# Small operands in PSUM, a norm queued behind a softmax, and another order in the second layer

## The chip, the cores and the metric

The kernel runs on one core of a Trainium2 chip. A core has TensorE (matrix products into PSUM), VectorE (elementwise work and reductions), ScalarE (activation functions), GpSimd[...] and SyncE, which issues most of the DMAs. In the profile they are called PE, DVE, ACT, POOL and SP; PEld are the weight loads of TensorE. The metric is the device time of one execution in microseconds (us).

## The reference

Four layers work in turn on one activation x of shape (2, 512, 32, 32), in 32-bit floats. The change touches the first two and the step into the third.

Layer 0 is a deformable attention with 8 heads of 64 channels, and a dense pair behind it. For each of the 2 x 8 pairs of batch and head, a small convolution of the queries gives offsets on an 8 x 8 grid; keys and values are sampled there, and the offsets also give the bias of the attention:

```python
off = gelu(conv(qg, off_dw_w) + off_dw_b)
off = tanh(einsum('bchw,oc->bohw', off, off_pw_w)) * 4.0
vx, vy = gx + off[:, 0], gy + off[:, 1]
nx, ny = 2.0 * vx / 7 - 1.0, 2.0 * vy / 7 - 1.0        # grid_kv
pos = grid_q[:, :, None, :] - grid_kv[:, None, :, :]
bias = sign(pos) * log1p(abs(pos))
bias = relu(bias @ cpb_w1 + cpb_b1)                    # 2 -> 128
bias = relu(bias @ cpb_w2 + cpb_b2)                    # 128 -> 128
bias = bias @ cpb_w3 + cpb_b3                          # 128 -> 1
sim = q @ k^T + bias;  out = softmax(sim) @ v
x = x + out_w @ out + out_b
x = x + mlp_w2 @ gelu(mlp_w1 @ bn(x) + mlp_b1) + mlp_b2
```

The bias is computed for every query (1024) and key (64) of every pair, with 128 hidden units: this is by far the largest part of the work.

Layer 1 is a linear attention: queries and keys (64 channels) are brought to unit length per position, k^T x and the sum of the keys are formed once per batch, and each position is divided by a sum over its query. Layer 2 begins with a group norm, whose means and variances are taken over x as layer 1 leaves it; layers 2 and 3 are softmax attentions.

## The kernel before, in words

**Layer 0.** The outer loop runs over u = 0 to 15, one head of one batch each. Within a u, o = 0 to 7 are groups of keys, and each o has two half steps. A half step is: VectorE makes the first hidden layer h1 with four operations (`first_hidden`, L705, each the sum of a table x and a table y); TensorE multiplies it by the second weights (`second_hidden`, L729) in four groups q = 0 to 3 of 16 products each, all of which read all four parts of h1; ScalarE applies bias and ReLU (L739, L741); GpSimd adds groups (L750, L753), and issues DMAs that add others. Later products reduce this to sim. The table y is written by VectorE (L690) into columns 0 to 255 of one single PSUM bank, `self.bank`, that layer 0 keeps for small things: the same bank has small statistics of the softmax (`self.joint`, columns 364 up), the product `o` of the offsets at columns 256 and 257, and now and then the sampling's weights and products.

Beside this stream, other generators are stepped at fixed places, one piece between two pieces of the stream: `attend` (bias plus q k^T, the softmax and its product with v, L785 to L869) and `offsets`, for a pair of heads at a time. There are eight such pairs; the first is computed at the start, the other seven beside u = 1, 3, 5, 7, 9, 11 and 13. The steps of `offsets` that the change touches are, in order: tanh on ScalarE (L421); three VectorE operations giving the positions of the keys and their distance from the queries, `pos` (L426, L427, L429); abs, log and sign on ScalarE (L444 to L446); on VectorE the product of log and sign (L451); a DMA of it on SyncE's queue; g on ScalarE (L457), and a DMA of it. The first pair (`bt == 0`) takes the sign in another way. The order of instructions on each engine is the order in which the generators issue them. The framework adds the waits; between different engines it treats one PSUM bank as a whole, whichever columns are touched.

**The tail of layer 0.** The last head's softmax is `attend` with u = 15: turn sim (L827), maximum (L828), four small copies (L825), L830, L831, subtract (L833), exp on ScalarE (L835), sum (L837), copies, reciprocal (L840), multiply (L842), turn (L844, into `pt`). TensorE multiplies `pt` by v (L855), copies bring it to `att` (L866, L869), and the projection follows (L255, and L895 for the last block). Then comes the dense pair, `mlp0`. It multiplies in seven products of half size, P1 to P7 (`seven`, L942), for which sums of the weights' blocks are made on GpSimd (`left_sums`) and sums of the right side's blocks on VectorE (`first_sums`, L925 and L926; `second_sums`). `norm(0)` scales x into blocks r0 to r3 with eight operations (L976) and then forms r4 and r5. In this part the framework's scheduler decides the places of `norm(0)` among the instructions around it; what follows, from the first product on, is in an order written out by hand.

**Layer 1.** The whole layer is issued in a hand-written order of helpers at L1278 to L1322, for TensorE, ScalarE and VectorE; GpSimd and SyncE are left to the scheduler. `queries_keys(b, half)` makes 16 products and an addition each (L1116, L1119) and squares after the second half (L1127). `means_less(b)` takes four negative means of x on ScalarE (L1132) into the tile `less`, cleared by a memset (L1099). `unit_length(b)` reduces, takes roots and scales (L1136 to L1141, giving `kn`). `turned_x` transposes x on TensorE (L1151), `keys_sum` sums the keys (L1160), `keys_x` forms k^T x (L1184), `centred` (L1201), `matrix` (L1224, L1234) and `result` (L1264, L1270) finish. `channel_means(2, 0, t)` (L1560, L1561), `group_means` (L1570 to L1580) and `norm_first` (L1611) already belong to layer 2's group norm; layer 2's first product, qk20P (L1428), needs what `norm_first` gives.

Of the kernel before, what the change touches and what calls it, by code (L numbers as in the profile page):

```python
# [56 lines left out]
class Net:  # L57
# [320 lines left out]
    def offsets(self, m, bt, ps):  # L378

        nc = self.nc
        b, t = divmod(bt, CT)
        if "q" not in m:
            self.normed(m, bt)
            yield
            self.queries(m, bt, ps)
            yield
        qp = m["q"]
        prod = self.fone.tile([P, 36 * NJ], F32, tag="big", name=f"prod{b}{t}")  # L390
        prod = prod.rearrange("p (a b j) -> p a b j", a=6, b=6)
        conv = self.fpool.tile([P, NJ], F32, tag="conv", name=f"conv{b}{t}")
        if bt == 0:
            yield from self.first_conv(qp, prod, conv, ps)
        else:
            for ky in range(6):
                nc.vector.tensor_tensor(
                    prod[:, ky, :, :].rearrange("p k (y x) -> p k y x", y=8),
                    self.window(qp, 6 * ky, 6),
                    self.taps[:, 6 * ky : 6 * ky + 6].unsqueeze(2).unsqueeze(3).to_broadcast([P, 6, 8, 8]),  # L400
                    ALU.mult,
                )
                if ky % 2:
                    yield
            for third in (slice(0, 24), slice(24, 44), slice(44, NJ)):
                nc.vector.tensor_reduce(
                    conv[:, third], prod[:, :, :, third].rearrange("p a b j -> p j (a b)"), AX.X, ALU.add
                )
                yield
        ge = self.fpool.tile([P, NJ], F32, tag="ge", name=f"ge{b}{t}")  # L410
        nc.scalar.activation(ge, conv, AF.Gelu, bias=self.col("dw_b"))
        if bt == 0:
            next(self.weights)
        yield
        yield from self.odd()
        o = self.bank[:, 256:258]
        for par in range(2):
            rows = slice(par * DH, (par + 1) * DH)
            nc.tensor.matmul(o[rows, :], lhsT=ge[rows, :], rhs=self.colr("pw", 2)[rows, :], start=True, stop=True)
        at = self.fpool.tile([P, 2], F32, tag="at", name=f"at{b}{t}")  # L420
        nc.scalar.activation(at, o, AF.Tanh)  # L421
        if bt == 0:
            early = self.fpool.tile([P, 1], F32, tag="early", name="early_ln")
            nc.scalar.activation(early, self.cols[:, 0:1], AF.Ln, scale=0.0, bias=1.0)
        yield
        nc.vector.scalar_tensor_tensor(at, at, 4.0, self.grid[:, G_KEY : G_KEY + 2], ALU.mult, ALU.add)  # L426
        nc.vector.tensor_scalar(at, at, 2.0 / 7.0, -1.0, ALU.mult, ALU.add)  # L427
        pos = self.fpool.tile([P, 2, W], F32, tag="pos", name=f"pos{b}{t}")
        nc.vector.tensor_tensor(  # L429
            pos,  # L430
            self.grid[:, G_QRY : G_QRY + W].unsqueeze(1).to_broadcast([P, 2, W]),
            at.unsqueeze(2).to_broadcast([P, 2, W]),
            ALU.subtract,
        )
        yield
        log = self.fpool.tile([P, 2, W], F32, tag="log", name=f"log{b}{t}")
        if bt == 0:

            nc.vector.scalar_tensor_tensor(log, pos, -1.0, pos, ALU.mult, ALU.max)
            nc.vector.tensor_scalar(pos, pos, 0.0, 2.0, ALU.is_ge, ALU.mult)  # L440
            next(self.weights)
            nc.scalar.activation(log, log, AF.Ln, bias=1.0)
        else:
            nc.scalar.activation(log, pos, AF.Abs)  # L444
            nc.scalar.activation(log, log, AF.Ln, bias=1.0)
            nc.scalar.activation(pos, pos, AF.Sign)  # L446
        yield
        if bt == 0:
            nc.vector.scalar_tensor_tensor(log, pos, -1.0, log, ALU.add, ALU.mult)
        else:  # L450
            nc.vector.tensor_tensor(log, log, pos, ALU.mult)  # L451
        logs = self.dram.tile([P, 2 * W], F32, tag="logs", name=f"logs{b}{t}")
        nc.sync.dma_start(logs, log.rearrange("p d x -> p (d x)"))
        spots = self.dram.tile([P, 2], F32, tag="spots", name=f"spots{b}{t}")

        g = self.fpool.tile([P, 2], F32, tag="g", name=f"g{b}{t}")
        nc.scalar.activation(g, at, AF.Identity, scale=W / 2.0, bias=self.grid[:, G_MID : G_MID + 1])  # L457
        nc.sync.dma_start(spots, g)
        m["log"], m["logs"], m["spots"] = log, logs, spots
        yield  # L460
# [343 lines left out]
    def attend(self, u, m, sim, att, ps):  # L804
# [36 lines left out]
        yield True  # L841
        nc.vector.tensor_tensor(t, t, joint.unsqueeze(2).to_broadcast([P, 2 * NB, W]), ALU.mult)  # L842
        pt = self.soft.tile([P, HF], F32, tag="pt", name=f"pt{u}")
        nc.vector.transpose(pt, t.rearrange("p a k -> p (a k)"))  # L844
        yield

        if ps:
# [15 lines left out]
        for c in range(2):  # L863
            at = slice(c * DH, (c + 1) * DH)
            if ps:
                nc.scalar.copy(to[:, :, c, :], o[at, :, 0 : HF // 2])  # L866
            else:
                nc.scalar.copy(to[:, 0, c, :], parts[0][at, :])
                nc.vector.tensor_copy(to[:, 1, c, :], parts[1][at, :])  # L869
        yield True  # L870

    def project_block(self, acc, att, w, bias: str, b: int, o: int, out):
# [74 lines left out]
    def mlp0(self):  # L947
# [5 lines left out]
        with ExitStack() as ctx:  # L953
# [16 lines left out]
            def norm(b):  # L970

                r = [xpool.tile([P, 2, HF], F32, tag=f"r{i}", name=f"mx{b}{i}") for i in range(7)]
                for i in (0, 3, 2, 1):
                    for k in range(2):
                        t = 2 * (i // 2) + k
                        vec.tensor_scalar(  # L976
                            r[i][:, k, :],
                            self.xs[b][t][:, (i % 2) * HF : (i % 2 + 1) * HF],
                            s2[:, t : t + 1],
                            self.col("bn2_b", t),  # L980
                            ALU.mult,
                            ALU.add,
                        )
                        yield r
                self.first_sums(vec, r)
                if b > 0:
                    self.second_sums(vec, r)
                yield r

            for xn in norm(0):  # L990
                pass
            ready = weights(0)
            with self.tc.manual_schedule(engines={getattr(mybir.EngineType, e) for e in ("PE", "Activation", "DVE")}):
                for n in range(B * CT):
# [86 lines left out]
    def layer1(self, w, bias):  # L1081
# [3 lines left out]
        with ExitStack() as ctx:  # L1085
# [10 lines left out]
            vec, act, gps = nc.vector, nc.scalar, nc.gpsimd  # L1096
            spare = pool.tile([P, N], F32, tag="spare", name="l1spare")
            less = pool.tile([P, CT, 32], F32, tag="less", name="l1less")
            gps.memset(less, 0.0)  # L1099
            pick = pool.tile([P, B], F32, tag="pick", name="l1pick")  # L1100
            gps.tensor_tensor(pick, self.ident[:, 0:B], self.ident[:, 32 : 32 + B], ALU.add)
            for at in (64, 96):
# [26 lines left out]
            def means_less(b):  # L1129

                for t in range(CT):
                    act.activation(spare, self.xs[b][t], AF.Copy, scale=-1.0 / N, accum_out=less[:, t, b : b + 1])  # L1132
# [145 lines left out]
            self.first = {2: self.first_block(2, 0)}  # L1278
            engines = {getattr(mybir.EngineType, e) for e in ("PE", "Activation", "DVE")}
            with self.tc.manual_schedule(engines=engines):  # L1280
                queries_keys(0, 0)
                means_less(0)
                queries_keys(0, 1)
                queries_keys(1, 0)
                unit_length(0)
                means_less(1)
                queries_keys(1, 1)
                keys_sum(0)
                turned_x(0, range(NB))
                unit_length(1)  # L1290
                divided(0)
                keys_x(0)
                row = means_row()
                turned_x(1, range(0, 4))
                centred(0)
                keys_sum(1)
                turned_x(1, range(4, NB))
                matrix(0)
                turned(0, 0)
                turned(0, 1)  # L1300
                means_columns(row)
                divided(1)
                for j in range(2):
                    for h in range(2):
                        result(0, j, h)
                keys_x(1)
                for t in (0, 2):
                    self.channel_means(2, 0, t)
                turned(1, 0)
                turned(1, 1)  # L1310
                centred(1)
                for t in (1, 3):
                    self.channel_means(2, 0, t)
                matrix(1)
                steps = self.group_means(2, 0, ps_m.tile([P, 2, 5 * CT], F32, tag="s", name="gm2"))
                result(1, 0, 0)
                next(steps)
                result(1, 0, 1)
                next(steps, None)
                result(1, 1, 0)  # L1320
                self.norm_first(2)
                result(1, 1, 1)  # L1322

# [790 lines left out]
```

## Time and profile before

| | |
|---|---|
| median of 3 runs | 3247.07 us (3243.41 to 3247.81) |
| profiled execution, its own time | 3249.37 us |
| span in the profile | 3247.6 us |
| TensorE busy | 3223.4 us (99%), mean granted clock 0.998 |
| VectorE busy | 2427.2 us (75%) |
| ScalarE busy | 1960.6 us (60%) |
| GpSimd busy | 2355.6 us (73%) |
| first bias product to last of layer 0's 16,384 | 23.2 to 1913.8 us |
| first product of the dense pair | 1954.84 us |
| first product of layer 2 | 2396.68 us |

Times inside the profile are counted from the start of its span, and the profiled execution's own time is 1.8 us longer than the span. A row of a group gives line, engine, operation, tiles written and read, shapes, count, and behind the first bar busy time in all and mean ns of one, behind the second the idle time just before and what ended it. In the timeline each row gives start, length, engine, line and tiles, and the idle time before it in brackets. The clock is the share of full speed that TensorE was granted.

### The profile page before, as it was taken

The page shows a single profiled execution, that of the slowest core. Times are in us where ns is not written, and L with a number is a line of the kernel's source. Part 1 is how long each engine was busy: PE and PEld are TensorE (multiplying, and loading weights), DVE is VectorE, ACT ScalarE, POOL GpSimd, SP SyncE. Part 2 cuts the span into 40 slices and gives each one's busy share as a digit, 9 for nine tenths or more (in the row PEclk, how much of TensorE's full clock was granted, in tenths as well). Part 3 has the DMA queues.
Part 4 walks back from the last instruction along what each step waited for, and adds up shares of the span by engine and source line. Part 5 has one row for each costly group of instructions (what it writes and reads, how often), then busy time and mean ns, then how long its engine had stood idle before and what let it go on. Part 6 is the DMA issues. An engine that isn't in the chain of part 4 may idle for free.

```text
span 3247.6 us, 58820 instructions
## 1 busy us (share of the span) xinstructions
PE 3223.4 (99%) x24188; PEld 1221.3 (38%) x24188; DVE 2427.2 (75%) x2745; ACT 1960.6 (60%) x2032; POOL 2355.6 (73%) x1559
## 2 busy tenths in 40 slices
PE   9999999999999999999999999999999999999999
PEld 4343323322233333333433334444555533455333
DVE  7878888878877678878877755575465689855897
ACT  7787887887877688887887742111131466213662
POOL 7999999999988699999989954433333458634575
PEclk9999999999999999999999999999999999999999
DMA  6787777777777577777877752111000100000001
GB/s 178 160 170 160 167 167 161 167 157 167 164 161 148 122 166 160 169 162 162 168 163 166 160 152 78 47 39 39 1 1 1 40 1 1 14 1 14 1 1 53
DMA packets 94349, 341.88 MB, mean 105 GB/s; under 512 B 16625, under 2 KB 18801, under 8 KB 78897
## 3 DMA queue, kind: packets, MB, share of 16 engines
q0 software_dynamic: 52832, 232.82, 37.2%
q1 hardware_dynamic: 40224, 103.06, 9.9%
q8 instruction: 195, 3.19, 0.4%
q10 hardware_dynamic: 1008, 2.08, 0.2%
q14 instruction: 90, 0.73, 0.1%
HBM read 67.36 MB, written 4.46 MB: 22 GB/s over the span
## 4 chain that ended last, share of the span: by engine, by line
PE 84%; DVE 10%; POOL 4%; issue 2%; ACT 1%; DMA 1%; DVEq 0%; POOLq 0%; ACTq 0%; SPq 0%
PE hp L729 46%; PE s L1653 5%; PE o L1682 5%; DVE h L705 3%; PE qk20P L1428 1%; PE qk30P L1428 1%; PE m_5P L942 1%; PE m_3P L942 1%; PE m_2P L942 1%; PE m_0P L942 1%; PE qk31P L1428 1%; PE qk21P L1428 1%; PE m_6P L942 1%; PE m_4P L942 1%; PE m_1P L942 1%
## 5 line engine op out<-in xcount | busy, mean ns | idle before, releaser
L729 PE MATMUL hp<-h,w2s 128*32 128x512 f32 x16384 | 1795.2, 592 | 2.1 <-DVE h L705 1.0
L705 DVE CUSTOM_DVE_ANT_1 h<-tx,bank 128x1024 f32<-128x1024 f32 (+1 forms) x1028 | 1180.8, 1212 | 261.8 <-PE hp L729 197.0
L739 ACT ACTIVATE h<-hp,magb 128x1024 f32<-128x1024 f32 x1024 | 1132.7, 1110 | 370.2 <-PE hp L729 368.5
L729 PEld LDWEIGHTS hp<-h,w2s 128*32 128x32 f32 x16384 | 558.6, 110 | 1200.2 <-issue 1123.7
L753 POOL TENSOR_TENSOR h<-h,h 128x1024 f32<-128x1024 f32 x254 | 723.9, 2850 | 0.0
L750 POOL TENSOR_TENSOR h<-h,h 128x1024 f32<-128x1024 f32 x255 | 718.7, 2818 | 1.5 <-ACT h L739 1.5
L1657 ACT ACTIVATE e<-s 128x1024 f32<-128x1024 f32 x256 | 261.8, 1024 | 181.1 <-PE s L1653 177.2
L746 POOL DMA_DIRECT2D h<-h x255 | 269.7, 1058 | 119.9 <-ACT h L739 116.3
L741 ACT ACTIVATE h<-h,flip 128x1024 f32<-128x1024 f32 x256 | 294.4, 1150 | 8.4
L1682 PE MATMUL o<-e,v 64*64 64x512 f32 x2048 | 265.3, 589 | 2.2 <-DVE q L1721 2.2
L1653 PE MATMUL s<-q,k 64*64 64x512 f32 x2048 | 266.0, 591 | 0.0
L1664 POOL TENSOR_TENSOR some<-some,e 128x1024 f32<-128x1024 f32 x64 | 167.7, 2620 | 26.4 <-ACT e L1657 23.8
L1662 POOL TENSOR_TENSOR some<-e,e 128x1024 f32<-128x1024 f32 x32 | 76.1, 2378 | 141.7 <-DVE sum L1671 102.4
L765 POOL DMA_DIRECT2D h<-h x124 | 141.5, 1141 | 21.0 <-DMA h<-h 19.2
L1669 DVE TENSOR_TENSOR sum<-sum,e 128x1024 f32<-128x1024 f32 x64 | 124.0, 1938 | 29.5 <-ACT e L1657 26.8
L912 POOL TENSOR_TENSOR mlp_w<-mlp_w 128x512 f32<-128x512 f32 x16 | 21.1, 1318 | 169.8 <-DMA mlp_w<-in_mlp_w 153.0
L755 POOL DMA_DIRECT2D h<-h x127 | 109.1, 859 | 39.0 <-POOL h L753 37.2
L1682 PEld LDWEIGHTS o<-e,v 64*64 64x64 f32 x2048 | 77.9, 133 | 145.0 <-issue 135.1
L1653 PEld LDWEIGHTS s<-q,k 64*64 64x64 f32 x2048 | 76.6, 133 | 133.1 <-issue 117.2
L1003 ACT ACTIVATE mh<-mh,cols 128x512 f32<-128x512 f32 x64 | 46.1, 721 | 124.3 <-DVE mh L1021 63.6
L1416 POOL TENSOR_TENSOR sq<-q 128x512 f32<-128x512 f32 x32 | 33.3, 1039 | 99.2 <-DVE q L1435 55.1
L1667 DVE TENSOR_TENSOR sum<-e,e 128x1024 f32<-128x1024 f32 x32 | 80.9, 2527 | 32.0 <-ACT e L1657 32.0
(583 smaller groups left out, 3328.1 us busy)
## 6 DMA issues: line engine op xcount, KB each, us to landing
h<-h POOLq DMA_DIRECT2D x382, 512.0 KB, 5.5
lb<-logs SPq DMA_DIRECT2D x63, 512.0 KB, 6.6
h<-h POOLq DMA_DIRECT2D x124, 256.0 KB, 3.7
sum<-h SPq DMA_DIRECT2D x248, 128.0 KB, 3.3
mlp_w<-in_mlp_w SPq DMA_DIRECT2D x16, 1024.0 KB, 4.9
x<-in_x SPq DMA_DIRECT2D x8, 512.0 KB, 7.9
qkw<-in_l_qk SPq DMA_DIRECT2D x2, 2048.0 KB, 7.9
out<-x SPq DMA_DIRECT2D x15, 256.0 KB, 2.0
```

What stands on the lines that cost most here:

```text
L705: self.nc.vector._custom_dve(TENSOR_ADD_SAT, out=h1[r][:, k, cut, :], in0=x[:, 4 * half + 2 * r + k, :].unsqueeze(1).to_broadcast([P, H // ...
L729: nc.tensor.matmul(hp[rows, cut], lhsT=self.l0w2[:, 32 * q : 32 * q + 32], rhs=h1[k][:, cut], start=True, stop=True)
L739: nc.scalar.activation(y, hp, AF.Relu, bias=self.magb[:, q, 0:1])
L741: nc.scalar.activation(y, y, AF.Copy, scale=self.flip)
L746: nc.gpsimd.dma_start(y, ys[0], accum_op=ALU.add)
L750: (nc.vector if final else nc.gpsimd).tensor_tensor(y, y, ys[2], ALU.add)
L753: (nc.vector if final else nc.gpsimd).tensor_tensor(z, z, other, ALU.add)
L942: self.nc.tensor.matmul(acc[p], lhsT=w[:, a, k, p * P : (p + 1) * P], rhs=right(r, k), start=k == 0, stop=k == 1)
L1653: nc.tensor.matmul(s[halves[c], par, :], lhsT=ks[p][rows, at : at + DH], rhs=qs[p][rows, cut], start=True, stop=True)
L1657: nc.scalar.activation(e, s, AF.Exp, scale=DH**-0.5)
L1664: nc.gpsimd.tensor_tensor(state["some"], state["some"], e, ALU.add)
L1682: nc.tensor.matmul(o[halves[par], r, :], lhsT=v[n // 2][rows, n % 2, at : at + DH], rhs=e[rows, par, :], start=(n == 0), stop=(n == NB - 1),)
```

## The change

There are three parts.

1. In `offsets`, the result of tanh and the tile `at` (scaled offset and key position) lie in `self.bank`, columns 258 to 261, and the sign lies there at columns 384 to 447, where the sampling's weights and products also lie at other times. VectorE's operations at L426, L427, L429 and L451 so read one operand from PSUM. `log` and `pos` stay in SBUF.
2. `norm(0)` of the dense pair is no longer free to be placed anywhere: its first two operations are issued behind the last softmax's turn (L844), the other six and the two sums behind VectorE's copy at L869.
3. In layer 1, the memset of `less` is on VectorE; `means_less(0)` comes first; half of `turned_x(0)` comes ahead of `keys_sum(0)`; the channel means of t = 1 come ahead of `turned(1)` and `centred(1)`; the first step of the group means comes ahead of the first `result(1)`, and `norm_first(2)` ahead of both `result(1, 1)`.

```diff
-        at = self.fpool.tile([P, 2], F32, tag="at", name=f"at{b}{t}")
-        nc.scalar.activation(at, o, AF.Tanh)
+        tanh, at = self.bank[:, 258:260], self.bank[:, 260:262]
+        nc.scalar.activation(tanh, o, AF.Tanh)
...
-        nc.vector.scalar_tensor_tensor(at, at, 4.0, self.grid[:, G_KEY : G_KEY + 2], ALU.mult, ALU.add)
+        nc.vector.scalar_tensor_tensor(at, tanh, 4.0, self.grid[:, G_KEY : G_KEY + 2], ALU.mult, ALU.add)
...
-            nc.scalar.activation(pos, pos, AF.Sign)
+            sign = self.bank[:, 384:448].rearrange("p (d x) -> p d x", d=2)
+            nc.scalar.activation(sign, pos, AF.Sign)
...
-            nc.vector.tensor_tensor(log, log, pos, ALU.mult)
+            nc.vector.tensor_tensor(log, log, sign, ALU.mult)
...
-        nc.vector.transpose(pt, t.rearrange("p a k -> p (a k)"))
+        self.weights_turned = nc.vector.transpose(pt, t.rearrange("p a k -> p (a k)"))
...
-                nc.vector.tensor_copy(to[:, 1, c, :], parts[1][at, :])
+                self.values_out = nc.vector.tensor_copy(to[:, 1, c, :], parts[1][at, :])
...
-            for xn in norm(0):
-                pass
+            first_norm = norm(0)
+            with self.tc.issue_after(self.weights_turned.ins):
+                for _ in range(2):
+                    next(first_norm)
+            with self.tc.issue_after(self.values_out.ins):
+                for xn in first_norm:
+                    pass
...
-            gps.memset(less, 0.0)
+            vec.memset(less, 0.0)
...
+                means_less(0)
                 queries_keys(0, 0)
-                means_less(0)
                 queries_keys(0, 1)
...
                 queries_keys(1, 1)
+                turned_x(0, range(0, 4))
                 keys_sum(0)
-                turned_x(0, range(NB))
+                turned_x(0, range(4, NB))
...
-                for t in (0, 2):
+                for t in (0, 2, 1):
                     self.channel_means(2, 0, t)
                 turned(1, 0)
                 turned(1, 1)
                 centred(1)
-                for t in (1, 3):
-                    self.channel_means(2, 0, t)
+                self.channel_means(2, 0, 3)
                 matrix(1)
                 steps = self.group_means(2, 0, ps_m.tile([P, 2, 5 * CT], F32, tag="s", name="gm2"))
+                next(steps)
                 result(1, 0, 0)
-                next(steps)
+                next(steps, None)
                 result(1, 0, 1)
-                next(steps, None)
-                result(1, 1, 0)
                 self.norm_first(2)
-                result(1, 1, 1)
+                for h in range(2):
+                    result(1, 1, h)
```

## The prediction

> **What bounds the kernel now.** I read the page's first, fourth and fifth parts, then the by-form groups of VectorE, then each of the three places in time.
>
> ```profile
> PE 3223.4 (99%) x24188; PEld 1221.3 (38%) x24188; DVE 2427.2 (75%) x2745; ACT 1960.6 (60%) x2032; POOL 2355.6 (73%) x1559
> PE 84%; DVE 10%; POOL 4%; issue 2%; ACT 1%; DMA 1%; DVEq 0%; POOLq 0%; ACTq 0%; SPq 0%
> L729 PE MATMUL hp<-h,w2s 128*32 128x512 f32 x16384 | 1795.2, 592 | 2.1 <-DVE h L705 1.0
> ```
>
> TensorE is the bound: 99% busy, 84% of the chain. Only what lets it start sooner, or run at full clock, counts. One half step of the offsets' bias (64 products L729) takes it 6.86 us, and VectorE's share of it is four L705 at about 1.15 us, 4.62 in all, so VectorE has 2.2 us over per half step.
>
> VectorE's groups with their forms (busy and mean ns behind the bar):
>
> ```profile
> L451 DVE TENSOR_TENSOR log<-log,pos 128x64 f32<-128x64 f32 x7 | 36.3, 5183 | 0.0
> L429 DVE TENSOR_TENSOR pos<-grid,at 128x64 f32<-128x64 f32 x8 | 21.7, 2712 | 0.3
> L426 DVE SCALAR_TENSOR_TENSOR at<-at,grid 128x2 f32<-128x2 f32 x8 | 6.9, 863 | 0.4 <-ACT at L421 0.4
> L831 DVE TENSOR_SCALAR bank<-bank,cols 128x16 f32<-128x16 f32 x16 | 3.9, 243 | 0.5
> ```
>
> An operation over 64 columns takes 5.2 us while L831 on 16 columns takes 0.24. Those two SBUF inputs wait for something. In u = 3, VectorE's timeline and then TensorE's L729 alone in four stretches of half a step (busy us, matmuls, weight loads, clock, DMA share, GB/s):
>
> ```profile
> 412.64 0.68 DVE L833 TENSOR_TENSOR t<-t,bank 128x512 f32<-128x512 f32 x1
> 413.24 7.17 DVE L451 TENSOR_TENSOR log<-log,pos 128x64 f32<-128x64 f32 x1
> 420.33 4.60 DVE L705 CUSTOM_DVE_ANT_1 h<-tx,bank 128x1024 f32<-128x1024 f32 x4
> ```
>
> ```profile
> 407.50:414.36 6.86, 6.86 (x68) 2.08 (x64) 1.00 0.89 205
> 421.23:428.09 6.86, 6.41 (x42) 1.43 (x42) 1.00 0.87 162
> 428.09:434.95 6.86, 6.86 (x72) 2.07 (x68) 1.00 0.57 135
> ```
>
> Behind the 7.17 the next h tile ends at 424.93; TensorE wants all four parts of it within 1.3 us of 421.23. It makes 42 products in the stretch, not 64: 22 x 0.107 = 2.4 us. From start to start the loss is 2.92.
>
> The tail of layer 0 and the clock of layer 1 (TensorE's timeline with the idle time before; stretches with the columns PE, weight loads, DVE, ACT, POOL, clock, DMA, GB/s; ScalarE's timeline):
>
> ```profile
> 1937.41 0.69 PE L855 MATMUL bank<-pt,v 64*64 64x256 f32 x2 [4.28 <-DVE pt L844]
> 1937.40:1944.00 6.60, 6.59 (x15) 2.68 (x16) 0.85 (x2) 0.73 (x2) 0.31 (x1) 0.53 0.68 242
> 2346.79 1.06 ACT L1132 ACTIVATE l1spare<-x 128x1024 f32<-128x1024 f32 x1 [27.17 <-POOL l1less L1099]
> 2355.12 2.28 PE L1160 MATMUL kb<-kn,l1ones 128*128 128x64 f32 x16 [1.29 <-DVE kn L1140]
> 2355.00:2362.20 7.20, 7.08 (x50) 6.95 (x50) 3.47 (x6) 6.40 (x11) 1.27 (x1) 0.76 0.01 2
> 2387.60:2396.70 9.10, 6.74 (x22) 2.79 (x21) 5.78 (x18) 3.20 (x6) 3.70 (x3) 0.81 0.00 0
> 2396.68 1.52 PE L1428 MATMUL qk20P<-xn,qkw 128*128 128x512 f32 x3 [1.20 <-DVE xn L1611]
> ```
>
> TensorE waits 4.28 us for the last softmax, then runs at 0.53 of its clock. In layer 1 it waits for kn, for the matrices and for the first xn, at 0.76 and 0.81.
>
> [...] GpSimd's sums L750 and L753 take 2.82 and 2.85 us and L451 takes 1.42 to 7.17; L429 of the first pair, with GpSimd not summing yet, takes 0.24, the later seven 3.07. [...] VectorE's L705, idle 23.8 us for ScalarE's L421 and 28.8 for L583, which share the bank with y. [...] The trace: half clock for 6.83 us (1936.78 to 1943.6) behind the 4.28, and for 3.41 twice in layer 1.
>
> **Part by part.**
>
> *Offsets (seven pairs; the eighth, the first in time, is at the start).* L426, L429 and L451 now have one input in SBUF and one in PSUM. I price them at the uncontended rows: 0.16, 0.24 and 0.24. VectorE loses (6.9 - 1.3) + (21.7 - 1.9) + (36.3 - 1.7) = 60 us of work, nearly all of it hidden under TensorE. What is not hidden, from the starts of the groups of 16 products beyond 1.716 us with no other matmul between: 1.59 in u = 1, and 0.44 + 2.48 in each of u = 3, 5, 7 and 13; none in 9 and 11. 1.59 + 4 x 2.92 = 13.3 us. This is the ceiling.
>
> The new waits: sign lies in the bank that y, h's input, lies in, so ScalarE's sign waits for the h tile before it, VectorE's next reader waits for sign, ScalarE's g waits for the log product, and the next h tile waits for g. Worked for u = 3: L426 to L429 end near 391.7 instead of 395.1. Sign ends at 402.2 as before (ReLU, abs, a table load of 1.28, Ln stand ahead of it), so h_210 runs 402.2 to 406.8, two us later than before; TensorE's limit is 407.5 + 1.3. The softmax group (2.6) and y (0.49) follow to 410.0; h_300 ends at 414.7, limit 415.7. The subtraction and the product end at 415.6, g at 416.05, h_310 at 420.7, limit 422.5. No stall is left. For u = 1, h_110 ends at 160.7 against 161.0; for u = 9 the y of the sixth step now waits for sign (1184.25) and h_600 ends at 1189.5 against 1189.4. I take 0.8 off for these two: **12.5**, range 5 (two thirds of a us lost at each h tile behind sign and g) to 13.3. The first pair's g00 now precedes TensorE's L320 in the same bank: at most 0.3, in the 0.8. On SP's queue, logs and spots of one pair change places with a sum DMA; they are wanted a whole u later.
>
> *The dense pair's norm.* Before, eight L976 (0.55 each) and the two sums L925/L926 (1.22 each) lie between the softmax's operations. Without them the chain from 1924.4 is 0.71 + 0.61 + 0.80 + 0.21 + 0.27 + 0.60 + 0.78 (exp) + 0.69 + 0.83 + 0.21 + 0.30 + 0.72 + 0.75 = 7.5, so pt is at 1931.9 instead of 1937.36, before TensorE is done with its ob products at 1932.98. The wait of 4.28 goes, and with it the half clock: 6.83 us at half rate are 3.4 us of work lost. Less 0.3 for the seam: **7.4**. The norm now runs after the copies (1934.9): six L976 to 1937.7, the residual additions L264 between, the sums after; r4 and r5 are wanted by P6 at about 1950, r0 by P1 at 1947.3. The weights' DMA on SP and GpSimd's left sums move forward with L855 (landing 4.8 us, then 4 x 1.32 by about 1944). If that cover fails, P1 or P6 waits, at most for what was gained. Bounds 4 (the half clock stays) and 8.
>
> *Layer 1.* Memset of less on VectorE instead of behind GpSimd's three sums of 2.35: means(0) can begin at 2340.5 instead of 2346.79 and is done before queries_keys(0, 1); sq0 follows the addition at 2347.4 instead of 2351.39. kn(0) is ready near 2353.4 instead of 2354.97, before TensorE ends its products at 2353.83; sixteen transposes then stand ahead of kb. keys_x(0) begins at about 2359.45 instead of 2362.17: 2.7, of which the half clock is 1.7. GpSimd's later pieces keep their order. In the second half, channel means of t = 1 come before m1c, so m1c is 0.26 later, but mat(1) no longer waits for those of t = 3, and norm_first precedes two of the four result groups on VectorE: first xn some 3.5 us sooner, now 2396.54. Sum **6.2**; 3 if an idle 1.3 us again brings the half clock (1.7), 7 at the most.
>
> *Sum.* 12.5 + 7.4 + 6.2 = 26.1. The profiled execution took 3249.37 us, 1.8 more than its span of 3247.6: 3223.3 there. The median of the runs is 3247.07, 2.3 below the profiled one: **3221.0**. Whether the median or the profiled time is the typical one is worth 2 us either way.
>
> **Rivals.** *The bank takes back [...]* (0.19; its extreme, that PSUM operands do not shorten the operations, included): waits for sign and g stall TensorE [...]. For it: seven pairs, and tables are loaded ahead of sign; against it: 2 us of slack behind sign in the working above. Then 7.4 + 6.2 = 13.6, 3233.5. *The tail only moves its wait* (0.11): P1 waits for weights or r tiles, or the clock stays half. For it: GpSimd's left sums and the norm both run in the 12 us ahead of P1; against: all are worked out done before 1947. Then 12.5 + 1.5 + 6.2 = 20.2, 3227. *Slower* (0.05): sign reaches the bank so late that every pair stalls. All gains with the ceiling are 13.3 + 7.4 + 6.2 = 26.9, so it decides from 26.9 / 7 = 3.8 us of stall per pair, which by the working for u = 3 needs sign 2.0 + 3.8 = 5.8 us later than 402.2, five ReLUs of 1.1 us ahead of it. At 5 us per pair: 3247.1 + 8 = 3255. *No change* (0.03): losses of the first and third kind cancel, near 3247.
>
> **How the numbers follow.** The likeliest case has 0.62: 3221, by itself 3216 to 3226. The range takes in the tail and the bank cases: 3215 to 3235. About 0.2% (6.5 us) is what a measurement of this kernel can tell from no change. Faster 0.91, same 0.04, slower 0.05.
>
> **What would show it.** The three VectorE groups at 0.16 to 0.3 us a piece; the stretch of u = 3 with 64 L729 products; VectorE's idle time before h for ScalarE's sign and g (some us per pair, hidden). TensorE's L855 with no idle time before it and the clock 1.00 until m_0P, which starts about 20 us sooner (12.5 + 7.4). In layer 1, kb and the first m at full clock and the first xn 6 us nearer to the end of the dense pair. The prediction is wrong if L429 or L452 stay above 1 us, if half steps behind sign are short of products, or if TensorE idles before m_0P.

## The result and the profile after

The changed kernel took 3222.53 us (median of 4 runs, 3221.20 to 3223.45) against 3247.44 us (median of 4, 3243.41 to 3248.85) for the kernel before: a ratio of 0.9925, 95% interval 0.9908 to 0.9942, that is 24.4 us less (19 to 30). The profiled execution took 3223.45 us, its span 3221.7.

The page of the changed kernel, parts 1, 4 and 5:

```profile
PE 3206.4 (100%) x24188; PEld 1218.9 (38%) x24188; DVE 2365.0 (73%) x2746; ACT 1958.2 (61%) x2032; POOL 2359.2 (73%) x1558
PE 90%; DVE 5%; POOL 2%; DMA 1%; issue 1%; ACT 0%; DVEq 0%; SPq 0%; POOLq 0%; ACTq 0%
L730 PE MATMUL hp<-h,w2s 128*32 128x512 f32 x16384 | 1784.1, 593 | 0.2
```

VectorE lost 62 us of busy time and half of its share of the chain; TensorE's matmuls are the same in number. Its idle time fell from some 24 us to 15, and its busy time by 17, since a product that waits for its input inside a group, or runs at half clock, counts as busy (in the stretches that the prediction shows, 42 products made 6.41 us of busy time at u = 3, and TensorE was busy for 6.59 of 6.60 us at 0.53 of its clock).

VectorE's groups with their forms, the operations that now read PSUM, and h with its idle time:

```profile
L429 DVE TENSOR_TENSOR pos<-grid,bank 128x64 f32<-128x64 f32 x8 | 1.8, 221 | 0.3
L452 DVE TENSOR_TENSOR log<-log,bank 128x64 f32<-128x64 f32 x7 | 1.5, 212 | 0.0
L706 DVE CUSTOM_DVE_ANT_1 h<-tx,bank 128x1024 f32<-128x1024 f32 x1020 | 1176.1, 1215 | 295.3 <-PE hp L730 197.6 <-ACT bank L447 31.3 <-ACT bank L584 28.4
```

L429 went from 2712 to 221 ns and the product from 5183 to 212. The wait for sign (L447) is there, 31.3 us ahead of h, and it costs next to nothing: TensorE alone (L730) in three stretches as long as a half step that cover the half steps of u = 3 around the product,

```profile
405.12:411.99 6.87, 6.87 (x68) 2.08 (x64) 1.00 0.75 160
411.99:418.85 6.86, 6.86 (x67) 2.01 (x63) 1.00 1.02 207
418.85:425.71 6.86, 6.86 (x68) 2.09 (x64) 1.00 0.62 137
```

has none that is short of products. Behind sign TensorE loses 0.15 us in u = 3 and at most 0.23 in any pair. The tail, layer 1 and the step into layer 2, from TensorE's timeline, and the stretch around L856 with its clock:

```profile
1920.69 0.43 PE L856 MATMUL bank<-pt,v 64*64 64x256 f32 x2
1935.12 10.46 PE L943 MATMUL m_0P<-mx,mlp_w 128*128 128x512 f32 x24
2335.69 1.90 PE L1166 MATMUL kb<-kn,l1ones 128*128 128x64 f32 x16
2370.84 9.68 PE L1434 MATMUL qk20P<-xn,qkw 128*128 128x512 f32 x22 [0.34 <-DVE xn L1617]
```

```profile
1915.00:1924.00 9.00, 9.00 (x29) 3.77 (x28) 7.14 (x18) 1.45 (x3) 0.00 (x0) 1.00 0.43 140
```

L856 starts with no idle time before it and takes 0.43 instead of 0.69, at a clock of 1.00 instead of 0.53. kb takes 1.90 instead of 2.28. Five marks on TensorE's line divide the gain (us from the span's start; the last row is the rest of the span):

| mark | before | after | gained in the stretch that ends there |
|---|---|---|---|
| last group of bias products starts | 1912.08 | 1899.69 | 12.39 |
| first product of the dense pair | 1954.84 | 1935.12 | 7.33 |
| first product of layer 1 | 2339.38 | 2319.65 | 0.01 |
| first k^T x product (keys_x) | 2362.17 | 2339.78 | 2.66 |
| first product of layer 2 | 2396.68 | 2370.84 | 3.45 |
| end | 3247.6 | 3221.7 | 0.06 |

The prediction had 12.5, 7.4, 2.7 and 3.5. The experiments ask whether these four numbers are what the edits are worth, or what they were worth in these two executions.

### The profile page after: what moved, and what is told of

It reads as the page before. It is cut to its first block, busy times and chain, and to the rows that moved or that the text cites. A ratio compares the mean times of both kernels' runs of the same rounds, so it can differ in the third digit from the quotient of the medians.

```text
span 3221.7 us, 58840 instructions
## 1 busy us (share of the span) xinstructions
PE 3206.4 (100%) x24188; PEld 1218.9 (38%) x24188; DVE 2365.0 (73%) x2746; ACT 1958.2 (61%) x2032; POOL 2359.2 (73%) x1558
## 4 chain that ended last, share of the span: by engine, by line
PE 90%; DVE 5%; POOL 2%; DMA 1%; issue 1%; ACT 0%; DVEq 0%; SPq 0%; POOLq 0%; ACTq 0%
PE hp L730 52%; PE s L1659 5%; PE o L1688 5%; PE qk20P L1434 2%; PE qk30P L1434 2%; PE qk31P L1434 1%; PE m_7P L943 1%; PE m_6P L943 1%; PE m_4P L943 1%; PE m_3P L943 1%; PE m_0P L943 1%; PE qk21P L1434 1%; PE m_5P L943 1%; PE m_2P L943 1%; PE m_1P L943 1%; DVE sum L1675 1%
## 5 line engine op out<-in xcount | busy, mean ns | idle before, releaser
L730 PE MATMUL hp<-h,w2s 128*32 128x512 f32 x16384 | 1784.1, 593 | 0.2
L730 PEld LDWEIGHTS hp<-h,w2s 128*32 128x32 f32 x16384 | 559.3, 110 | 1187.0 <-issue 1126.4
```

Source lines behind the costliest of these rows:

```text
L730: nc.tensor.matmul(hp[rows, cut], lhsT=self.l0w2[:, 32 * q : 32 * q + 32], rhs=h1[k][:, cut], start=True, stop=True)
```

## The experiments

**Each part alone.** Theory: the parts add up. Rival: they lean on each other, through the clock or the bank's waits. Each kernel is the one before with the hunks of one part; the diffs are those of the change.

offsets_only: 

> The kernel before with the first part alone (offsets' operands in PSUM). By the theory that the parts are independent: the last group of bias products starts 12.4 us sooner (1912.08 becomes about 1899.7), everything behind it as in the kernel before, so about 3247 - 12.4 = 3235. If the parts lean on each other, for example because the tail starts with another state of the clock, the difference is off by over 2 us. If the bank's new waits cost much and the tail had made up for it, the last bias product moves by less than 10 us.

norm_only: 

> The kernel before with the second part alone (norm queued behind the last softmax). Independent parts: the last bias product where it was (1912.1), the first product of the dense pair at 1954.84 - 7.3 = 1947.5 with the clock full throughout, so about 3247 - 7.3 = 3240. If the gain of the tail came from the first part's timing, it is under 5 us.

layer1_only: 

> The kernel before with the third part alone (order of layer 1, memset on VectorE). Independent parts: the dense pair begins at 1954.8 as before, the stretch from there to layer 2's first product shrinks from 441.84 to about 435.7 us, so about 3247 - 6.1 = 3241. If the half clock of layer 1 depended on what came before, a stretch near 438 to 440.

| kernel | last bias group | from there to the dense pair | from there to layer 2 | median of runs | ratio to before (95%) |
|---|---|---|---|---|---|
| before | 1912.08 | 42.76 | 441.84 | 3244.91 | |
| offsets_only | 1897.92 | 41.99 | 439.10 | 3232.26 | 0.9956 (0.9940 to 0.9973) |
| norm_only | 1909.11 | 35.41 | 439.10 | 3236.31 | 0.9968 (0.9957 to 0.9980) |
| layer1_only | 1913.19 | 42.09 | 435.73 | 3241.52 | 0.9988 (0.9977 to 0.9999) |
| changed | 1899.69 | 35.43 | 435.72 | 3222.53 | 0.9925 (0.9908 to 0.9942) |

(Median of before: of the runs beside the three; the last row's ratio is against its own.) Each stretch takes the value of the changed kernel where its part is in, to 0.02 us in the tail and layer 1 and to 1.8 us in the bias stretch, so the parts don't lean on each other by more than that. But columns move where nothing was edited: the bias stretch by 4.1 us between norm_only and layer1_only, the same offsets by the 1.8 us between offsets_only and the changed kernel (most of it is a wait that the last experiment looks at), and layer 1 by 2.74 between the kernel before and offsets_only or norm_only. The kernel before had a share of chance in its profile.

**Which operand.** offsets_only in two halves: the sign alone, and tanh with `at` alone.

```diff
 # sign_only
-            nc.scalar.activation(pos, pos, AF.Sign)
+            sign = self.bank[:, 384:448].rearrange("p (d x) -> p d x", d=2)
+            nc.scalar.activation(sign, pos, AF.Sign)
...
-            nc.vector.tensor_tensor(log, log, pos, ALU.mult)
+            nc.vector.tensor_tensor(log, log, sign, ALU.mult)
 # tanh_only
-        at = self.fpool.tile([P, 2], F32, tag="at", name=f"at{b}{t}")
-        nc.scalar.activation(at, o, AF.Tanh)
+        tanh, at = self.bank[:, 258:260], self.bank[:, 260:262]
+        nc.scalar.activation(tanh, o, AF.Tanh)
...
-        nc.vector.scalar_tensor_tensor(at, at, 4.0, self.grid[:, G_KEY : G_KEY + 2], ALU.mult, ALU.add)
+        nc.vector.scalar_tensor_tensor(at, tanh, 4.0, self.grid[:, G_KEY : G_KEY + 2], ALU.mult, ALU.add)
```

sign_only: 

> The kernel before with only the sign in PSUM (L451 has one SBUF input; L426 and L429 keep two). [...] the product takes 0.2 us instead of 5.2 on the mean, L429 stays at 3.07. The four steps at u = 3, 5, 7 and 13 lose nothing any more, the 1.59 at u = 1 stays: the last bias product starts 11 to 12 us sooner. Rival, that the gain needs the earlier start of the whole chain of small operations: under 8 us.

tanh_only: 

> The kernel before with only tanh and at in PSUM (L426, L427 and L429 have one SBUF input; the sign and its product stay in SBUF). [...] L426 and L429 take 0.14 and 0.22, the product stays at about 5. Only the 1.59 at u = 1 goes: the last bias product starts 1 to 2 us sooner. The wait of g for the bank comes without the gain of the product, so 0 is possible too. Rival as for the sign alone: over 4 us.

sign_only: product 0.21, L429 still 2.72, last bias group at 1899.60 (12.5 sooner), 3232.59 us, ratio 0.9968 (0.9952 to 0.9984). At u = 1 it still lost 0.98. tanh_only: L429 0.22, product 5.39, last bias group at 1909.74 (2.3 sooner), 3244.10 against 3243.41, ratio 1.0004 (0.9989 to 1.0020). So nearly all of the first part's gain is the one product L451; the others, 25 us less work, are worth 1 to 2 us, most of it at u = 1, and can't be told from nothing in the runs.

**Is it GpSimd's sums?** One more product with two SBUF inputs in the changed kernel:

```diff
             nc.vector.tensor_tensor(log, log, sign, ALU.mult)
+            nc.vector.tensor_tensor(pos, log, pos, ALU.mult)
```

> The changed kernel with one more product of 128x64 behind L452, both inputs in SBUF, its result not used. [...] it takes some 1.4 to 7.2 us beside GpSimd's sums although its only difference to L452 (0.21) is the place of one input, and the loss of 2.9 us each at u = 3, 5, 7 and 13 comes back: the last bias product is some 11 us later than in the changed kernel. Rival, that the long time of before was a wait for ScalarE or for the semaphores around sign: the second product takes about 0.2 us and nothing is lost.

VectorE's groups by form, and its timeline and GpSimd's at u = 3:

```profile
L453 DVE TENSOR_TENSOR pos<-log,pos 128x64 f32<-128x64 f32 x7 | 13.6, 1945 | 0.2
L452 DVE TENSOR_TENSOR log<-log,bank 128x64 f32<-128x64 f32 x7 | 1.5, 212 | 0.0
```

```profile
414.53 1.70 DVE L453 TENSOR_TENSOR pos<-log,pos 128x64 f32<-128x64 f32 x1
```

```profile
413.18 2.95 POOL L755 TENSOR_TENSOR h<-h,h 128x1024 f32<-128x1024 f32 x1
416.95 0.84 POOL L767 DMA_DIRECT2D h<-h  x1 [0.82 <-DMA h<-h]
```

Half of what was expected holds: of two neighbours that differ in the place of one input, one takes 0.21 us and the other 0.53 to 4.63. At u = 3 the slow one ends at 416.22, GpSimd's sum at 416.13. The other half failed: the loss did not come back (3223.31 us, last bias group at 1899.57). The second product met a sum that had begun 1.35 us before and sat through that one alone; 1.7 us fit into VectorE's slack. Only at u = 9 did it sit through two sums (4.63 us), and there TensorE lost 0.49 us. So what made 7.17 out of a 2.85-us sum? GpSimd in the kernel before, at the same place:

```profile
412.79 1.02 POOL L647 TENSOR_SCALAR tx<-lb,cols 128x512 f32<-128x512 f32 x1
413.51 1.15 POOL L746 DMA_DIRECT2D h<-h  x1
414.13 2.95 POOL L753 TENSOR_TENSOR h<-h,h 128x1024 f32<-128x1024 f32 x1
416.54 1.34 POOL L765 DMA_DIRECT2D h<-h  x1
417.14 3.17 POOL L750 TENSOR_TENSOR h<-h,h 128x1024 f32<-128x1024 f32 x1
```

L451 had stood since 413.24, beside L647 at first; it did not get its turn before the sum at 414.13 either. The next sum came 0.06 us behind the first, and L451 waited for that too: it ended at 420.40, 0.09 behind the second. In all nine kernels here with such a product, 63 of 63 end 0.089 to 0.095 us behind the end of a GpSimd sum.

**Opening the gap.** If the loss is the second sum, it should go without moving any operand, by something between the two sums:

```diff
             elif q == 3:
+                if u % 2 and o == 2 and half == 1:
+                    gap = self.fpool.tile([P, 16], F32, tag="gap", name=f"gap{u}")
+                    for _ in range(6):
+                        nc.gpsimd.memset(gap, 0.0)
                 (nc.vector if final else nc.gpsimd).tensor_tensor(y, y, ys[2], ALU.add)
```

> The kernel before with six small memsets (128x16, nobody reads them) on GpSimd ahead of one of its sums, the L750 of o = 2, second half, in odd u: the sum that follows on L753 while L451 waits at u = 3, 5, 7, 11 and 13. No operand moves. In the traces each long L451 ends 0.09 us behind the end of a GpSimd sum, and it sits through a second sum where that begins 0.35 us or less behind the first (7.2 us), and not where the gap is 0.40 or more (3.6 to 4.3). [...] the five products take about 4.3 us or less, the losses of 2.92 at u = 3, 5, 7 and 13 go, and the last bias product starts some 11 us sooner than 1912.1, though nothing was taken from VectorE. [...] Rival, that GpSimd's added 0.6 us come back as a stall of the stream: less than 8 us gained.

VectorE's and GpSimd's timelines at u = 3:

```profile
413.59 3.62 DVE L451 TENSOR_TENSOR log<-log,pos 128x64 f32<-128x64 f32 x1
```

```profile
414.16 2.96 POOL L757 TENSOR_TENSOR h<-h,h 128x1024 f32<-128x1024 f32 x1
417.23 0.84 POOL L769 DMA_DIRECT2D h<-h  x1
417.80 0.40 POOL L753 MEMSET gap<- 128x16 f32 x1
```

L451 passes 0.09 us behind the first sum; the six memsets then take until 419.0, where the next sum begins. No product takes over 4.05 us, no half step at u = 3, 5, 7, 11 or 13 is short, and the last bias group starts at 1899.91, 12.2 us sooner, with 23.1 us of L451 still on VectorE. The runs: 3234.17 us, ratio 0.9980 (0.9972 to 0.9988) to a kernel before that was at 3241.63 beside it: some 6.5 us, less than the profile's 12.2. They reach from 3232.41 to 3240.70, so the memsets may not have spared the product every time; these runs have no trace. Profile and runs agree on the direction, though not on the size: it was never the 60 us of work, and not the 5.2-us product as such, but the second sum. The limits of 0.35 and 0.40 us in the expectation did not hold in general: products sat through a second sum that came up to 0.36 us behind the first (tanh_only), and others passed in gaps of 0.28 (u = 1) or, behind a second sum, of 0.2. What decides who goes first stays open.

This also tells the chance in the kernel before. Pairs that lost 2.9 us, and the last bias group:

| profile | pairs hit | last bias group |
|---|---|---|
| layer1_only | 4 (u = 3, 7, 11, 13) | 1913.19 |
| before; memset_only | 4 (u = 3, 5, 7, 13) | 1912.08; 1912.23 |
| tanh_only | 4 | 1909.74 |
| filled_wait; norm_only | 3 | 1909.96; 1909.11 |
| filled_short | 1 | 1904.01 |
| opened_gap; sign_only | 0 | 1899.91; 1899.60 |

Over all its timed runs the kernel before lies between 3233.83 and 3252.16 us, the changed one between 3221.17 and 3224.10. Most of the scatter went with the product: offsets_only lies between 3230.60 and 3233.54 (4 runs), sign_only between 3231.32 and 3235.70 (5), tanh_only, which keeps the product, between 3234.74 and 3252.47 (10).

**The tail: wait or clock?** Products that nobody reads, in the wait of the kernel before:

```diff
         else:
             parts = [self.bank[:, 0 : HF // 2], sim[:, 0 : HF // 2]]
+        if u == 2 * BP - 1:
+            for _ in range(16):          # filled_short: 8
+                nc.tensor.matmul(
+                    sim[:, 256:512], lhsT=self.ident, rhs=att[0][:, 0:256], start=True, stop=True
+                )
```

filled_wait: 

> The kernel before with 16 products of 128x256 that nobody reads put on TensorE's queue just ahead of the last head's L855, where it waits 4.28 us. They take 16 x 0.22 = 3.5 us and are over before pt comes. Theory that the tail's gain of 7.3 is two things, the wait and the clock: the wait stays (pt is not sooner), but the clock does not fall, and the dense pair's first product comes about 3.4 us sooner than 1954.84. Rival, that the products behind pt were slow for another reason, such as the DMA share of 0.68 there: the first product stays near 1954.8.

filled_short: 

> As filled_wait with 8 products of 128x256 in the wait instead of 16. Sixteen took 7.0 us and held up L855 by 2.6; eight take 3.5 and are over before pt. The clock stays full; L855 starts with pt as in the kernel before (4.3 us behind the last ob product); from there to the first product of the dense pair 14.4 us instead of 17.43, so 3.0 us are the clock's part of the tail's 7.3. Rival: no better than the kernel before, since the clock falls all the same.

In filled_wait the sixteen took 7.07 us, twice what I had reckoned, since the trace has two instructions for each (x32), and ended 2.6 us behind pt; the clock stayed at 1.00, and the dense pair began 42.30 us behind the last bias group. The runs: 3241.61 against 3244.07, ratio 0.9992 (0.9983 to 1.0001). filled_short has the wait as before, from TensorE's timeline:

```profile
1924.90 3.62 PE L854 MATMUL sim<-att,ident 128*128 128x256 f32 x16
1929.33 0.43 PE L860 MATMUL bank<-pt,v 64*64 64x256 f32 x2 [0.82 <-DVE pt L844]
1943.76 12.61 PE L947 MATMUL m_0P<-mx,mlp_w 128*128 128x512 f32 x29
```

From L860 to m_0P 14.43 us, as in the changed kernel (1920.69 to 1935.12) and in filled_wait, against 17.43 before. Of the tail's 7.33 us in this pair of profiles, 3.00 are the clock and 4.3 the wait. The clock's part is not a constant: with the old tail, from the last bias group to the dense pair, the profiles lie between 41.18 (sign_only) and 42.76 us (before), against 39.75 here, so 1.4 to 3.0. The runs don't show it (3241.74 against 3241.63, ratio 1.0001, 0.9992 to 1.0010, which leaves room for a gain of 2.6 us at the most). In this profile layer 1 had its half clock again (441.86, as before, instead of 439.1): of eight profiles with the old layer 1, two have it and six don't, with the same instructions.

The clock records show what differs. The half clock comes in stretches of 3.41 us or, at the old tail, also of 6.83. In the kernel before these start at 1936.778, 2356.618 and 2390.751: the distances are 123.0 and 10.0 times 3.413 us. At the old tail, sign_only and opened_gap got one such length (41.18 and 41.46 us), the other five two (41.99 to 42.76). In layer 1 the two profiles that lost got it 17.24 and 17.57 us behind its first product. In the six that didn't, idle times as long left the clock at 1.00. So it looks like a draw; what decides it no run shows.

**Layer 1: which edit?**

```diff
-            gps.memset(less, 0.0)
+            vec.memset(less, 0.0)
```

> The kernel before with only the memset of less moved from GpSimd to VectorE, no instruction in another order. Theory: the first half's gain is this memset: means(0) on ScalarE starts about 6 us sooner, sq0 and kn(0) follow, keys_x(0) begins 2 us or more sooner than 2362.17 and the clock does not fall there; the second half keeps its waits and its half clock. Rival, that the transposes ahead of the keys' sum carry the gain: keys_x(0) within 1 us of 2362.17 or the half clock still there.

From layer 1's first product to keys_x: 22.80 us before (21.65 in the profiles without half clock), 20.13 with the memset alone, 20.12 with the whole change. The memset is the whole first half; moving means_less and the transposes adds 0.01. ScalarE's timeline shows it:

```profile
2340.42 1.06 ACT L1132 ACTIVATE l1spare<-x 128x1024 f32<-128x1024 f32 x1 [20.94 <-DVE l1less L1099]
```

From keys_x to layer 2: 34.51 before (32.9 without half clock), 32.92 here, 31.07 with the whole change: the second half's order is worth 1.84. In the runs 3241.45 against 3243.41, ratio 0.9993 (0.9986 to 1.0000).

The mean clock that each run lists tells more than these medians. With the old layer 1 and no half clock at the tail in the profile (norm_only, filled_wait, filled_short) it is 0.999 in 17 of 29 runs and 1.000 in 12; with the new layer 1 and tail (the changed kernel, second_product, spots_early) it is 1.000 in all 17. With the old tail, memset_only and layer1_only have 0.999 in all 28, while the kernel before, beside all these runs, has 0.998 or 0.997 in 24 of 89. This points to a half clock in layer 1 in a good part of the executions, which the memset alone takes away.

**A new wait, and a try to beat it.** In the profile of the changed kernel u = 9 loses 1.15 us at its last half step, and 0.8 follow at u = 10: VectorE idles 7.01 us at L572 for the DMA of `at`, issued at 1184.13. Moving g and its DMA ahead of the logarithm:

```diff
             ALU.subtract,
         )
         yield
+        spots = self.dram.tile([P, 2], F32, tag="spots", name=f"spots{b}{t}")
+        g = self.fpool.tile([P, 2], F32, tag="g", name=f"g{b}{t}")
+        nc.scalar.activation(g, at, AF.Identity, scale=W / 2.0, bias=self.grid[:, G_MID : G_MID + 1])
+        nc.sync.dma_start(spots, g)
...
-        spots = self.dram.tile([P, 2], F32, tag="spots", name=f"spots{b}{t}")
-        g = self.fpool.tile([P, 2], F32, tag="g", name=f"g{b}{t}")
-        nc.scalar.activation(g, at, AF.Identity, scale=W / 2.0, bias=self.grid[:, G_MID : G_MID + 1])
-        nc.sync.dma_start(spots, g)
```

after_again: 

> The changed kernel itself, as the measure for the next one on the same chip: 3222 to 3224.

spots_early: 

> The changed kernel with g and its DMA (spots) moved from behind the log product to behind pos, so ahead of abs, log and sign. In the changed kernel the first hidden tile behind u = 9's sampling waits until 1195.46 for a DMA of at (issued 1184.13), and TensorE loses 1.15 us there and 0.8 at the step into u = 10. Theory: with spots issued some 20 us sooner the DMA of at is sooner too, and 1.5 to 2 us come off: about 3221. Rival, that the late landing is the DMA queues' load at that place, whatever the time of issue, or that SyncE's queue holds the DMA of at in its old place: no gain, within 0.5 us. If g beside abs delays sign by 0.3 us per pair, no loss, since two us of slack lie behind it.

The changed kernel again: 3222.08 us, ratio 0.9934 (0.9920 to 0.9947). With spots early: 3223.11, ratio 0.9934 (0.9921 to 0.9948). No gain. The DMA of `at` was issued at 1176.99 instead of 1184.13 and VectorE didn't wait for it; but in the second profile of the unedited changed kernel the DMA, issued at 1183.25, came in time as well (2.16 us of idle time, no loss on TensorE). The 2 us were that execution's. And with g ahead of sign six pairs lose 0.30 to 0.38 us each, where the changed kernel loses 0.15 to 0.23 at those, and the stretch of u = 1 is 1.5 us longer: I had expected no loss.

## Why the prediction was right

Forecast 3221.0 in 3215 to 3235; measured 3222.53.

*Offsets, 12.5; measured 12.39,* by two errors that cancel. The step-by-step times for u = 3 hold once everything is set 1.43 us earlier (the stretch gained at u = 1): h_210 was worked out to start at 402.2 and started at 400.75, h_300 to end at 414.7 and ended at 413.29, h_310 to end at 420.7 and ended at 419.13. The bank's waits for sign and g stayed inside the slack, as worked out, but for the 0.15 us, and the first rival, that they take the gain back, fell with them. That one input from PSUM brings L426, L429 and L451 to 0.16, 0.24 and 0.24 us was my estimate; in the kernel before only operations such as L833 (one input from the bank, 0.68 us in all sixteen) spoke for it. They took 0.17, 0.22 and 0.21. The 0.8 taken off for u = 1 and u = 9 had a wrong reason and was too small: nothing is lost behind sign at u = 9; u = 1 lost 0.23, and 2 us went to the DMA of `at` in this execution. The step that failed there is "they are wanted a whole u later": at u = 9 `at` is wanted within the same u, some 11 us after g (g at 1177.67, VectorE free for L572 at 1188.44).

What was mis-sized is the loss of a hit pair: the whole of u = 3 takes 118.46 us before and 115.12 after, 3.34 and not 2.92. The working counted only groups with no other product between; behind them a half step with other products shrinks too (from 8.40 to 7.81 us). So "1.59 + 4 x 2.92 = 13.3 us", called the ceiling, is none: against the same profile of before, offsets_only gains 14.2 and the changed kernel's second profile 14.7. The four pairs gave 13.4 together and u = 1 gave 1.4; the DMA of `at` took 2.2 back in the first profile.

What the working did not see is that four hit pairs are a draw. It took the product's time (1.42 to 7.17) as given for each place. Where a row of seven equal operations spreads from 1.4 to 7.2 us, the gain from removing it spreads as well.

*Tail, 7.4; measured 7.33,* in norm_only 7.35. pt came 0.9 us before TensorE was through with the ob products (predicted 1.08). That the half clock goes with the wait was my estimate from one profile; the changed kernel has 1.00 there. The clock's part was put at 3.4 and is 3.00 here: the 6.83 us at half clock began at 1936.78, 0.63 us before the wait ended at 1937.41, and cost nothing until then. The wait's 4.3 is as read.

*Layer 1, 6.2; measured 6.12.* Right in sum and partly by luck. Of the 6.12, 2.74 are the half clock that this profile of before had in layer 1 and six of the eight with that layer 1 have not, so they are a gain only in a part of the executions; 1.52 are the memset, 1.84 the order of the second half. The step that put 1.7 of the first half's 2.7 on the clock measured 1.15. The transposes ahead of keys_sum were credited with filling TensorE while kn was made; memset_only shows that nothing had to be filled.

*Profile against median.* The prediction took 2 us off for the step from the profiled execution to the median and called that the uncertainty. The kernel before has medians from 3241.63 to 3247.44 in five sets of runs, and its first profile has near the most of everything: four hit pairs and two half clocks in layer 1. Against a later set the changed kernel gains 22.0 us in the medians (3222.08 against 3244.07; 21.4 by the ratio 0.9934), four less than the 26.1 forecast. 3221 was met because the 3247.07 that it started from lay 3 us above that later median as well; that is luck. "Slower" needed 3.8 us of stall per pair; none lost over 0.25 on TensorE behind sign.

## What to carry to other kernels

Look for a short VectorE operation that takes many times the time of its neighbours and ends each time a fixed bit behind a GpSimd operation (here 5.18 us on the mean, and 0.09 us behind a sum). Here one operand from PSUM brought it to 0.21 us, and six memsets in the row of GpSimd's sums to 4.05 at most in the one profile; the first was the surer. Count the places where it is late, not the busy time. Before a row of the profile is priced as gain, look whether the operations in it spread: the spread of 1.42 to 7.17 us here meant that one profile was a draw, so take a second. When several edits come together, one memset may be most of a part, so try the smallest edit alone.

## What the runs showed of the hardware

The VectorE product of 128x64 with two SBUF inputs (L451) sat through two GpSimd sums in a row at u = 3, 5, 7 and 13 of the kernel before, 6.92 to 7.18 us for the 0.21 us that it took with one input in PSUM. This happened with the second sum up to 0.36 us behind the first (tanh_only), though not at every such gap (0.28 at u = 1). In the profile with six memsets of 128x16 between the sums it passed after the first, in 3.62 us at u = 3. In all 63 cases it ended 0.089 to 0.095 us behind the end of a sum. The prediction had its 1.42 to 7.17 us beside GpSimd's sums; it did not allow for losing twice in a row.

TensorE's clock fell to half in layer 1 in two of eight profiles of the same instructions, for 3.41 us at a time, behind idle times of 1.0 to 1.3 us; in the other six, idle times as long left the clock at 1.00. The half-clock stretches in the kernel before began 123.0 and 10.0 times 3.413 us apart. Behind the 4.28 us of the last softmax the clock fell too (0.53), and not where 3.62 us of products that nobody reads were put in (1.00, with 0.82 us of wait left).
